# Layer 1's s1 of each edge's query as a 513th column of the gathered q row, instead of a broadcast through DRAM, and column sums over one column in 32

## Chip, cores and metric

One core of a Trainium2 chip runs the kernel. The metric is the time of one execution on the device in microseconds, as the median of several runs. TensorE (PE) multiplies matrices, VectorE (DVE), ScalarE (ACT) and GpSimd (POOL) work on tiles in SBUF, SyncE (SP) and POOL issue DMAs, and 16 DMA engines move the data.

## What is computed

Two graph layers on 32 batches of 512 nodes with 512 features, in float32. One adjacency matrix serves all batches; an entry is 1 with probability 1/128, so a node has about four neighbours. Layer 0 is attention with 8 heads of 64 over a node's neighbours; layer 1 is additive attention.

```python
    # layer 0
    h = jnp.maximum(_layernorm(x, axis=-1), 0.0)
    q, k, v = (h @ W + b for each), split into 8 heads
    attn = softmax(q k^T / 8 where adj, else -1e9);  x = x + (attn v) @ Wo + bo
    # layer 1
    h = jnp.maximum(_layernorm(x, axis=-1), 0.0) @ W
    s1, s2 = h @ a[:512], h @ a[512:]
    e = leaky_relu(s1[:, :, None] + s2[:, None, :], 0.2) * adj
    x = x + elu(softmax(e) @ h + beta * h)
```

Layer 1's softmax runs over all 512 nodes, and where adj is 0 the exponent is 0. So each row is the plain sum of all h (weight 1 each) plus, for the few edges, h weighted by exp(e) - 1.

## The kernel before

**Tiles.** A batch has T = 4 tiles of P = 128 nodes, sorted by the number of neighbours, so that the edges of a tile fill NG = 4 groups of 128 edge slots. For each group of slots the kernel gathers by indirect DMA (issued on POOL) one row for each edge: from a table `tab` in DRAM the neighbour's k, v and, for layer 1 of the batch two before (LAG = 2), the neighbour's s2 and normed features hn (`kv<-tab`, L925; a row is 1552 floats); and from `qtab` the query's q row (`qe<-qtab`, L945; 512 floats). Matrices of 0 and 1 (`OH`) with 32 columns a group bring sums over edges back to nodes.

**Layer 0, for a tile.** `qe` is multiplied by the k part (L976), summed over heads (L979), exponentiated (L985), and v is weighted by it on ACT (L990). PE sums edges to nodes (`px<-kv,OH`, L963), DVE divides (L1014), four transposes (L731) and the product with Wo (L41) follow, then the residual (L1029), the norm, relu into `hx` (L750), and two dot products with the rows of a (L1037): s2 into column 0 of `hx`, which goes to `tab` of the batch two later (L1043), and s1 into a column of the tile `s1`.

**self_sums, once a batch** (L1049). PE adds up `hx` over nodes with weights of 1/32 in 32 columns, so that each sum stands 32 times (L1057), ACT copies that (L1061), PE turns it (L731), and DVE adds up 128 columns for each quarter of the features (L1063, 128x512 to 128x4). For s1, PE turns the tile `s1` (L1066), ACT copies it (L1068), SP writes 512 floats to DRAM (`row`, L1069) and reads them back on all 128 partitions (`q<-row`, L1074) into a buffer of the ring `q`. DVE then picks each edge's s1: a product with OH (L1078) and a sum over 32 columns (L1079) give `s1e`, a column for each of the 16 groups of the batch.

**Layer 1's weights** (`edge_weights`, two batches later). DVE adds `s1e` and the gathered s2 for each half of the groups (L1095), applies the leaky slope (L1098), ACT takes exp (L1100), DVE subtracts 1 (L1101), copies it into the slots (L1105) and spreads it over OH (L1107, `wv`); PE sums with it (`pd<-kv,wv`, L963).

**Stage A, six tiles ahead.** x is fetched, normed, turned; k and v of two tiles come from seven half products (L837), and q from `queries`: product with Wq (L41), bias on DVE (L784), and a store by SP (L876). In batch 0 plain products make k and v (L802 to L811), and q, k and v are stored by indirect DMAs on POOL (L878), which need the nodes' places, worked out at the start.

**Order.** `Plan` builds the list of all operations once, each with an engine, an estimated duration, a due time (`key`; a tile is S = 20 units) and the buffers that it reads and writes. `Plan.order` then simulates the engines: at each step it takes, on the engine that can start first, the ready operation with the lowest key; an operation that needs a ring buffer waits for a free one, and rings other than PSUM's are handed out in order of key. PE gets a small bias to stay with the same width of weights (`STAY`), and DMAs are modelled as one pipe. The order that comes out is written down for each engine, and engines run it strictly in order. So a buffer less, a duration or a dependency more can move operations elsewhere. Rings that matter here: `q` 2 (also used for `q<-row`), `k` 2, `qe` 2 (both used by each tile), `kv` 5, `s1` 2.

Of the kernel before, what the change touches and what calls it, by code (L numbers as in the profile page):

```python
# [33 lines left out]
ROW = HO + HW_  # L34
LAG = 2
# [180 lines left out]
def kernel(  # L216
# [49 lines left out]
    def ring(n, shape, name):  # L266
# [8 lines left out]
        "q": ring(2, [P, D], "q"),  # L275
        "k": ring(2, [P, D], "k"),
        "v": ring(5, [P, H, VW], "v"),
        "kv": ring(5, [P, 2, ROW], "kv"),
        "qe": ring(2, [P, 2, D], "qe"),
# [12 lines left out]
        "s1": ring(2, [P, T], "s1"),  # L292
# [7 lines left out]
        "qtab": [dram.tile([N + 1, D], F32, name=f"qtab{i}", tag=f"qtab{i}") for i in range(3)],  # L300
# [27 lines left out]
    def setup():  # L328
        nc.gpsimd.iota(OH.bitcast(I32), pattern=[[1, D]], base=1, channel_multiplier=0)
        nc.gpsimd.iota(idx[:, 0, 0:1], pattern=[[1, 1]], base=0, channel_multiplier=1)  # L330
        make_identity(nc, ident)
        nc.gpsimd.memset(mhalf, -0.5)
        nc.vector.memset(rings["qe"][-1], 0.0)
        nc.vector.memset(one32, 1.0 / G)
        for b in rings["hx"]:
            nc.vector.memset(b[:, D:], 0.0)
        for b in rings["v"]:
            nc.vector.memset(b[:, :, HD:], 0.0)
        for b in [rmax, dmax, fin]:
            nc.vector.memset(b, 0.0)  # L340

    def constants():

        def load(fn, dma=4096, w=()):
            op("SP", 0.1, 20.0, fn, w=w, dma=dma)

        for dst, src in ((bk_r, bk), (bq_r, bq)):
            load(lambda dst=dst, src=src: nc.sync.dma_start(dst, bcast_rows(src, D)), P * D * 4, [C_["rows"]])
        load(lambda: nc.sync.dma_start(beta_b, bcast_rows(beta, 1)))
        zero = rings["qe"][-1].rearrange("p a b -> p (a b)")  # L350
        for tag, n in (("tk", D), ("tkv", D), ("qtab", D), ("th", HW_), ("tab", ROW)):
            for tab in rings[tag]:
                for c0, c1 in ((0, D), (HO, ROW)) if tag == "tab" else ((0, n),):
                    m = 1 if tag == "qtab" else DUMMY
                    load(lambda tab=tab, c0=c0, c1=c1, m=m: nc.sync.dma_start(
                        tab[N:, c0:c1], zero[:m, : c1 - c0]))
        for dst, src in ((bq_c, bq), (bk_c, bk)):
            load(lambda dst=dst, src=src: nc.sync.dma_start(
                dst, bass.AP(tensor=src.tensor, offset=src.offset, ap=[[1, P], [P, C]]),
                allow_slow_non_contiguous=True))  # L360
# [418 lines left out]
    def queries(b, t, key, hT):  # L779
# [4 lines left out]
        op("DVE", 0.7, key, lambda: nc.vector.tensor_tensor(q.ap, p.ap, bq_r, op=ALU.add), r=[p, C_["rows"]], w=[q])  # L784
# [128 lines left out]
    def stage_b(b):  # L913
# [16 lines left out]
        for t in range(T):  # L930
# [11 lines left out]
            if s is not None:  # L942
                qs = [buf("qe", f"qe{b}_{t}_{i}") for i in range(2)]
                for g in range(NG):
# [4 lines left out]
                       r=[s["qtab"], C_["qidx"]], w=[(qs[g // 2], g % 2)], dma=P * D * 4)  # L949
            wvb = edge_weights(b - LAG, t, kb, slots, held) if old is not None else None  # L950
# [17 lines left out]
    def layer0(b, t, kb, slots, held, qs, weights):  # L968

        s = st[b]  # L970
        for i in range(2):
# [3 lines left out]
            def mult(qe=qe, sl=sl):  # L975
                nc.vector.tensor_tensor(qe.ap, qe.ap, sl.ap[:, :, KO : KO + D], op=ALU.mult)  # L976

            def total(qe=qe, sb=sb):
                nc.vector.tensor_reduce(  # L979
                    sb.ap, qe.ap.rearrange("p n (h f) -> p n h f", f=HD), axis=AX.X, op=ALU.add  # L980
                )
# [10 lines left out]
            op("DVE", 1.24, key, mult, r=use([sl], [held[i]], "K"), w=[qe])  # L992
            op("DVE", 1.2, key, total, r=[qe], w=[sb])
# [55 lines left out]
    def self_sums(b, key):  # L1049
# [5 lines left out]
        def col_sums():  # L1055
# [5 lines left out]
        op("ACT", 0.6, key, lambda: nc.scalar.copy(csr.ap, pc.ap), r=[pc], w=[csr])  # L1061
        op("PE", 0.45, key + 0.49 * S, lambda: turned(pt.ap, csr.ap), r=[csr], w=[pt])
        op("DVE", 0.69, key + 0.5 * S, lambda: nc.vector.tensor_reduce(  # L1063
            cs.ap, pt.ap.rearrange("p (c q) -> p c q", c=C), axis=AX.X, op=ALU.add), r=[pt], w=[cs])
# [9 lines left out]
        op("SP", 0.1, key, lambda: nc.sync.dma_start(s1b.ap, row.ap.unsqueeze(0).to_broadcast([P, N])),  # L1074
           r=[row], w=[s1b], dma=P * N * 4)

        def pick():
            nc.vector.tensor_tensor(s1b.ap, OH, s1b.ap, op=ALU.mult)  # L1078
            nc.vector.tensor_reduce(  # L1079
                s1e.ap.rearrange("p t g -> p (t g)"), s1b.ap.rearrange("p (s r) -> p s r", r=G), axis=AX.X, op=ALU.add  # L1080
            )

        op("DVE", 1.4, key + 0.8 * S, pick, r=[C_["OH"]], w=[s1b, s1e])
        op("DVE", 0.2, key + 0.9 * S, lambda: nc.vector.scalar_tensor_tensor(
            fin, s["mv1"].ap[:, :, 0:2], 0.0, fin, op0=ALU.mult, op1=ALU.add), r=[s["mv1"]], w=[C_["fin"]])
        op("DVE", 0.2, key + 0.9 * S, lambda: nc.vector.tensor_tensor(rmax, rmax, s["rd"].ap, op=ALU.max),
           r=[s["rd"]], w=[C_["rmax"]])

    def edge_weights(b, t, kb, slots, held):
# [4 lines left out]
        for i in range(2):  # L1094
            op("DVE", 0.2, k1, lambda i=i: nc.vector.tensor_tensor(  # L1095
                z.ap[:, 2 * i : 2 * i + 2], s["s1e"].ap[:, t, 2 * i : 2 * i + 2], slots[i].ap[:, :, HO], op=ALU.add),
               r=[s["s1e"], *use([slots[i]], [held[i]], "H")], w=[z])
# [318 lines left out]
```

## Time and profile before

| | |
|---|---|
| runs shown | 2753.82, 2757.61, 2750.27 us; median 2753.82 |
| profiled execution | 2739.4 us, of which the span of the program 2737.2 |
| instructions in the span | 40002 |
| DMA | 242339 packets, 796.71 MB, mean 291 GB/s |
| granted TensorE clock | 0.988 in the mean |

How to read it: busy time is that of an engine's instructions without waits. Matmuls are pipelined and their ends modelled, so one product's duration (0.6 us for 128x512) is longer than the distance to the next one's start (0.43 us). "Idle before" is time of an engine ahead of an instruction, with what ended it. A line number is that of the kernel before. In a timeline line: start, duration, engine, line, operation, output and inputs, count.

### The profile page before, as it was taken

What the parts mean: (1) busy time and instruction counts of PE and PEld (TensorE: products, weight loads), DVE (VectorE), ACT (ScalarE), POOL (GpSimd) and SP (SyncE); (2) the same over time, 40 slices, a digit from 0 to 9 for tenths busy, and PEclk for the clock granted to TensorE, in tenths of its full rate; (3) what the DMA queues carried; (4) which work ended last, traced back from release to release, by engine and by line L of the source; (5) the groups of instructions that cost most, each with busy time, mean ns of one, the idle gap of its engine ahead of it and who ended that gap; (6) DMA issues with size and microseconds to landing.
All of it is one profiled execution on the core that took longest, in us unless ns stands there. A gap on an engine that the chain in (4) does not pass through costs nothing.

```text
span 2737.2 us, 40002 instructions
## 1 busy us (share of the span) xinstructions
PE 2662.8 (97%) x10250; PEld 1213.1 (44%) x10250; DVE 2093.0 (76%) x5138; ACT 1937.7 (71%) x6241; POOL 1835.0 (67%) x1730
## 2 busy tenths in 40 slices
PE   8899999999999999999999999999999999999986
PEld 4344444444444444444444444444444444444332
DVE  7667777777878777877877787777787787787763
ACT  1565777777778777777777777777777777777763
POOL 3787667666767676766766666666666676665663
PEclk9999999999999999999999999999999999999988
DMA  5889889888889888888888988988888898888963
GB/s 182 217 278 325 289 299 318 290 302 313 306 293 331 288 297 317 303 304 298 309 305 291 324 297 295 323 287 305 318 299 299 302 308 307 296 315 286 305 209 111
DMA packets 242339, 796.71 MB, mean 291 GB/s; under 512 B 35587, under 2 KB 35715, under 8 KB 242102
## 3 DMA queue, kind: packets, MB, share of 16 engines
q0 software_dynamic: 157056, 643.94, 69.8%
q1 hardware_dynamic: 85046, 150.15, 14.9%
q8 instruction: 83, 1.36, 0.2%
q14 instruction: 154, 1.26, 0.1%
HBM read 624.70 MB, written 169.26 MB: 290 GB/s over the span
## 4 chain that ended last, share of the span: by engine, by line
PE 91%; ACT 2%; DMA 2%; issue 2%; POOL 1%; DVE 1%; SPq 0%; POOLq 0%; DVEq 0%; ACTq 0%
PE pd L41 48%; PE pd L837 26%; PE pd L731 6%; PE pd L963 4%; PE px L963 4%; ACT kv L990 1%; DMA qe<-qtab,qidx 1%; PE pd L897 1%; PE pd L1057 1%; POOL kv L925 1%; DMA x<-in_x_dram,perm 0%; DMA kv<-tkv,idx 0%; POOL qe L945 0%; ACT hx L750 0%; DMA x<-in_adj_dram 0%
## 5 line engine op out<-in xcount | busy, mean ns | idle before, releaser
L990 ACT ACTIVATE kv<-kv 128x64 f32<-128x64 f32 x4096 | 1009.6, 335 | 6.0
L945 POOL DMA_INDIRECT qe<-qtab,qidx x512 | 544.7, 1064 | 245.2 <-issue 104.9
L925 POOL DMA_INDIRECT kv<-tab,idx x480 | 518.9, 1081 | 175.8 <-issue 111.0
L41 PE MATMUL pd<-wo,oT 128*128 128x512 f32 x1032 | 476.2, 605 | 6.0 <-ACT oT L1027 5.8
L41 PE MATMUL pd<-w,gT 128*128 128x512 f32 x1024 | 465.4, 597 | 4.0 <-ACT gT L1148 4.0
L41 PE MATMUL pd<-wq,hT 128*128 128x512 f32 x1024 | 465.1, 597 | 0.0
L756 POOL DMA_INDIRECT x<-in_x_dram,perm x252 | 355.6, 1411 | 82.6 <-issue 48.4
L976 DVE TENSOR_TENSOR qe<-qe,kv 128x1024 f32<-128x1024 f32 x256 | 312.0, 1221 | 30.8 <-DMA qe<-qtab,qidx 13.9
L41 PEld LDWEIGHTS pd<-wo,oT 128*128 128x128 f32 x1032 | 198.5, 194 | 254.1 <-issue 228.5
L979 DVE TENSOR_REDUCE s<-qe 128x16 f32<-128x1024 f32 x256 | 310.3, 1214 | 0.9
L41 PEld LDWEIGHTS pd<-w,gT 128*128 128x128 f32 x1024 | 195.4, 192 | 249.8 <-issue 235.1
L41 PEld LDWEIGHTS pd<-wq,hT 128*128 128x128 f32 x1024 | 195.6, 192 | 246.4 <-issue 244.5
L761 POOL DMA_INDIRECT out_dram<-w,perm x128 | 139.1, 1087 | 185.7 <-DVE w L1163 133.8
L743 POOL TENSOR_TENSOR mv<-mv,mhalf 128x1 f32<-128x1 f32 x256 | 176.0, 689 | 126.0 <-DVE mv L740 89.8
L837 PE MATMUL pd<-wk,hT 128*128 128x512 f32 x496 | 238.6, 606 | 1.4 <-ACT hT L776 1.4
L837 PE MATMUL pd<-wt,S 128*128 128x512 f32 x496 | 237.6, 601 | 1.6 <-DVE k L845 0.9
L837 PE MATMUL pd<-wv,S 128*128 128x512 f32 x496 | 233.3, 593 | 0.2 <-DVE v L845 0.2
L1157 ACT ACTIVATE w<-pd,dn 128x512 f32<-128x512 f32 x128 | 87.5, 684 | 152.4 <-PE pd L41 152.1
L1029 DVE TENSOR_TENSOR x<-pd,x 128x512 f32<-128x512 f32 x128 | 88.2, 689 | 129.6 <-PE pd L41 123.5
L738 DVE BATCH_NORM_STATS2 st<-x 128x6 f32<-128x512 f32 x256 | 176.5, 689 | 7.4 <-DMA x<-in_x_dram,perm 3.4
L1037 DVE CUSTOM_DVE_ANT_0 w<-hx,wa_r 128x512 f32<-128x512 f32 x256 | 175.9, 687 | 4.9 <-ACT hx L750 3.9
L731 PE MATMUL pd<-ident,w 128*128 128x128 f32 x1152 | 154.2, 276 | 25.6 <-DVE w L1014 14.0
(201 smaller groups left out, 3579.4 us busy)
## 6 DMA issues: line engine op xcount, KB each, us to landing
qtab<-q SPq DMA_DIRECT2D x124, 256.0 KB
tab<-hx SPq DMA_DIRECT2D x120, 260.0 KB
tab<-v SPq DMA_DIRECT2D x120, 260.0 KB
tab<-k SPq DMA_DIRECT2D x120, 256.0 KB
qe<-qtab,qidx POOLq DMA_INDIRECT x512, 6.7
q<-row SPq DMA_DIRECT2D x32, 256.0 KB
kv<-tab,idx POOLq DMA_INDIRECT x480, 7.7
x<-in_x_dram,perm POOLq DMA_INDIRECT x252, 7.3
```

The source lines that it names most:

```text
L41: nc.tensor.matmul(out, lhsT, rhs, start=start, stop=stop)
L731: nc.tensor.transpose(p[:, ts(c, P)], src[:, ts(c, P)], ident)
L738: nc.vector.bn_stats(s6.ap, src.ap)
L743: op("POOL", 0.75, key, lambda: nc.gpsimd.tensor_tensor(mv.ap[:, t, 2:3], mv.ap[:, t, 2:3], mhalf[:, 0:1], op=ALU.pow), w=[(mv, t)])
L756: nc.gpsimd.indirect_dma_start(dst, None, rows, bass.IndirectOffsetOnAxis(ap=perm[:, t : t + 1], axis=0), **lim)
L837: nc.tensor.matmul(p.ap, lhs()[:, c, :], rhs[:, c, :], start=first and c == 0, stop=c == K2 - 1, skip_group_check=True)
L925: nc.gpsimd.indirect_dma_start(dst, None, tab.ap, bass.IndirectOffsetOnAxis(ap=idx[:, t, g : g + 1], axis=0), bounds_check=N + DUMMY - 1, ...
L945: op("POOL", 1.3, kb - 0.84 * S + 0.1 * g, lambda q=qs[g // 2], g=g, t=t: nc.gpsimd.indirect_dma_start(q.ap[:, g % 2, :], None, s["qtab"]. ...
L963: nc.tensor.matmul(out(g), lhs(g), slots[g // 2].ap[:, g % 2, c0 : c0 + n], start=True, stop=True)
L976: nc.vector.tensor_tensor(qe.ap, qe.ap, sl.ap[:, :, KO : KO + D], op=ALU.mult)
L979: nc.vector.tensor_reduce(sb.ap, qe.ap.rearrange("p n (h f) -> p n h f", f=HD), axis=AX.X, op=ALU.add)
L990: nc.scalar.activation(p[:, h, 0:HD], p[:, h, 0:HD], AF.Copy, scale=p[:, h, HD : HD + 1])
```

## The change

`queries` of batch b copies a column of `s1` of batch b - 2 beside q, so that a row of `qtab` has 516 floats (q, s1, three unused zeros), and the gather that brings an edge's q brings its s1 too. `edge_weights` adds that column instead of `s1e`. The last two batches, whose layer 1 runs with no layer 0 beside it, keep the old way (`spread_s1`, a function of its own). The plan's bookkeeping treats q and the s1 column of a gathered row as parts. Ring `k` has one buffer instead of two, `s1` three instead of two. `self_sums` scales the column sums by 32 in ACT's copy and then takes one column in 32, 16 in all, for the sum. The two small operations on `fin` and `rmax` stand earlier in the text, with the same keys.

```diff
+QW = 516
-        "q": ring(2, [P, D], "q"),
-        "k": ring(2, [P, D], "k"),
+        "q": ring(2, [P, QW], "q"),
+        "k": ring(1, [P, D], "k"),
-        "qe": ring(2, [P, 2, D], "qe"),
+        "qe": ring(2, [P, 2, QW], "qe"),
-        "s1": ring(2, [P, T], "s1"),
+        "s1": ring(3, [P, T], "s1"),
-        "qtab": [dram.tile([N + 1, D], F32, ...
+        "qtab": [dram.tile([N + 1, QW], F32, ...
...
-        op("DVE", 0.7, key, lambda: nc.vector.tensor_tensor(q.ap, p.ap, bq_r, op=ALU.add), r=[p, C_["rows"]], w=[q])
+        op("DVE", 0.7, key, lambda: nc.vector.tensor_tensor(q.ap[:, 0:D], p.ap, bq_r, op=ALU.add), r=[p, C_["rows"]], w=[(q, "q")])
+        if b >= LAG:
+            s1 = st[b - LAG]["s1"]
+            op("DVE", 0.1, key, lambda: nc.vector.tensor_copy(q.ap[:, D : D + 1], s1.ap[:, t : t + 1]),
+               r=[(s1, t)], w=[(q, "s1")])
...
-            op("DVE", 1.24, key, mult, r=use([sl], [held[i]], "K"), w=[qe])
-            op("DVE", 1.2, key, total, r=[qe], w=[sb])
+            op("DVE", 1.24, key, mult, r=[(qe, "use"), *use([sl], [held[i]], "K")], w=[qe.q])
+            op("DVE", 1.2, key, total, r=[(qe, "use"), qe.q], w=[sb])
...
-        op("ACT", 0.6, key, lambda: nc.scalar.copy(csr.ap, pc.ap), r=[pc], w=[csr])
+        op("ACT", 0.6, key, lambda: nc.scalar.activation(csr.ap, pc.ap, AF.Copy, scale=float(G)), r=[pc], w=[csr])
-        op("DVE", 0.69, key + 0.5 * S, lambda: nc.vector.tensor_reduce(
-            cs.ap, pt.ap.rearrange("p (c q) -> p c q", c=C), axis=AX.X, op=ALU.add), r=[pt], w=[cs])
+        op("DVE", 0.2, key + 0.5 * S, lambda: nc.vector.tensor_reduce(
+            cs.ap, pt.ap[:, 0 :: G].rearrange("p (c q) -> p c q", c=C), axis=AX.X, op=ALU.add), r=[pt], w=[cs])
+        if b + LAG >= B:
+            spread_s1(b, key)
...
+    def spread_s1(b, key):
...
         for i in range(2):
-            op("DVE", 0.2, k1, lambda i=i: nc.vector.tensor_tensor(
-                z.ap[:, 2 * i : 2 * i + 2], s["s1e"].ap[:, t, 2 * i : 2 * i + 2], slots[i].ap[:, :, HO], op=ALU.add),
-               r=[s["s1e"], *use([slots[i]], [held[i]], "H")], w=[z])
+            def add(i=i):
+                s1 = s["s1e"].ap[:, t, 2 * i : 2 * i + 2] if qs is None else qs[i].ap[:, :, D]
+                nc.vector.tensor_tensor(z.ap[:, 2 * i : 2 * i + 2], s1, slots[i].ap[:, :, HO], op=ALU.add)
+
+            op("DVE", 0.2, k1, add, r=[*([s["s1e"]] if qs is None else [(qs[i], "use"), qs[i].s1]),
+                                       *use([slots[i]], [held[i]], "H")], w=[z])
```

## The prediction

> **What bounds the kernel now.** I read the page first, then the busy times by stretch, then TensorE's timeline in one late batch, then the waits of the tiles that the change touches.
>
> ```profile
> PE 2662.8 (97%) x10250; PEld 1213.1 (44%) x10250; DVE 2093.0 (76%) x5138; ACT 1937.7 (71%) x6241; POOL 1835.0 (67%) x1730
> PE 91%; ACT 2%; DMA 2%; issue 2%; POOL 1%; DVE 1%; SPq 0%; POOLq 0%; DVEq 0%; ACTq 0%
> ```
>
> TensorE is busy 97% of the span and carries 91% of the chain that ended last. A share of the whole span can hide stages, so the stretches come next (time; then busy us of PE, PEld, DVE, ACT, POOL; then clock, DMA share, GB/s).
>
> ```profile
> 0.00:100.00 100.00, 85.00 (x255) 41.82 (x256) 73.43 (x216) 24.02 (x49) 46.85 (x53) 0.93 0.60 171
> 200.00:300.00 100.00, 93.59 (x352) 40.72 (x351) 71.51 (x168) 60.60 (x199) 70.26 (x68) 0.98 0.89 309
> 1500.00:1800.00 300.00, 300.00 (x1208) 138.35 (x1200) 237.62 (x577) 222.54 (x713) 204.22 (x193) 1.00 0.87 302
> 2500.00:2600.00 100.00, 93.04 (x373) 40.81 (x372) 71.23 (x174) 71.67 (x241) 62.70 (x58) 0.95 0.87 297
> 2600.00:2680.00 80.00, 64.63 (x254) 27.23 (x253) 52.16 (x148) 51.08 (x163) 51.62 (x48) 0.89 0.69 208
> 2680.00:2737.00 57.00, 35.13 (x116) 13.88 (x114) 18.13 (x61) 17.34 (x41) 18.95 (x19) 0.85 0.31 94
> ```
>
> From 1500 to 1800 TensorE has no idle time. All its idle time is 2737.2 - 2662.8 = 74 us: 26.7 before 300 (15.0 + 5.3 + 6.4), 44.2 after 2500 (7.0 + 15.4 + 21.9), about 3 between. So work taken off any other engine can be felt in two places, the start and the tail; between them only TensorE's own work and its order count.
>
> Order counts because products with 32 columns of weights (L963, L897, L1057) and full ones do not follow each other for free. The first L1057 of each batch marks a period: from 1097.6 to 2473.9, 17 batches, each is 80.96 us within 0.02, with 8 changes between the two kinds. The batches from 362.2 to 608.3 last 81.7 to 82.3 us with 12 changes. A change costs about (82.0 - 80.96) / 4 = 0.26 us.
>
> **What is removed, added and moved.** The sum is made against the profiled execution (2739.4 us, span 2737.2); the median of the runs shown, 2753.8, is 14.4 above it, and I put the difference on the median.
>
> *TensorE.* For 30 of 32 batches the transpose of s1 goes.
>
> ```profile
> L1066 PE MATMUL pd<-ident,s x32: 271/272/273, 196.0 to 2668.4; 128*4 128x128 f32 x32
> 1098.62 0.27 PE L1066 MATMUL pd<-ident,s 128*4 128x128 f32 x1
> 1098.72 0.60 PE L731 MATMUL pd<-ident,x 128*128 128x128 f32 x4
> ```
>
> Its duration of 0.27 us is not what it costs: the next product starts 0.10 to 0.11 us later, products being pipelined. 30 x 0.11 = **-3.3 us**, on the path, since TensorE is full around each.
>
> *VectorE.* Gone: 30 picks of 0.685 + 0.686 (L1078, L1079), 41.1 us; and 32 sums of hn, 0.684 each, now over 16 columns instead of 512. The nearest row for that is L613's reduction of 256 columns, 0.42, and a 128x4 operation, 0.16: I take 0.2, so 32 x 0.48 = 15.5 us. Added: 120 copies of one column, 0.16 by L1105's copy of two columns: 19.2. Net -37 us of 2093, worth nothing between 300 and 2500, where PE does not wait for DVE.
>
> *ScalarE, SyncE.* 30 copies of 0.25 and 60 DMA issues go, 30 of which make SP's queue wait for the row to land (90.0 us in all). The scaled copy of the column sums (L1061) stays at L904's 0.60 against 0.59. Nothing, under the same cover; if the cover went, ACT at 71% has room.
>
> *DMA.* 30 broadcasts of 256 KB go, 7.9 MB of 796.7. All 640 stores and gathers of q carry 16 B more a row: 1.3 MB. What a gathered row of 2064 B costs is not in the trace. In one early stage rows of 2048 B (kv<-tk) land after 5.7 us and rows of 2080 B (kv<-tv) after 5.6, so nothing is one end; the other is a tenth more on the q gathers, the gap between the 6.7 us of a qe gather and the 7.4 of the kv gathers with their threefold rows. I take nothing, by the nearer row. TensorE's cover here is thick: a qe gather is followed by its product on DVE 4 to 15 us after it has landed.
> Against the change speaks the Trainium skill, DMA: Bandwidth & Descriptors, How a descriptor splits into AXI transactions: a read that does not start on a 256 B boundary fetches from the boundary below it. By that a row at a step of 2064 B takes an estimated 68.5 beats of 32 B on average instead of 64, 7% more on the q gathers; the sum stays as it is as long as the cover holds.
>
> *The new wait.* The z additions (L1095) now read the q buffer, so they wait for the qe gather too, and the next gather into that buffer waits for them. Behind them in DVE's order stand exp, L1101, L1105 and L1107, and then PE's L963. In the late batches this is free: the four tiles of the batch at 1101 make their second addition at 1126.5, 1150.4, 1164.7 and 1191.4, and their last gather, issued 6.7 us before it lands, is there at 1121.9, 1134.8, 1163.0 and 1175.7. The weights are ready 10 to 19 us before PE takes them. In batches 2 to 9 the additions run up to 9.3 us ahead of the gather, and the slack behind them is 2 to 20 us; in seven tiles it is short, by 0.1 to 4.8, together 12. PE has other products there, so this changes order, not work. Nor does the added column wait: L784 writes q 16 to 19 us after the L1037 that makes its s1 (1095.1 against 1076.7). One buffer for k holds too: a k is stored at 1115.45 and the next written at 1124.74, 9.3 us for a store whose like, the gathers, land in 7.7.
>
> In those nine batches, 362.2 to 1097.6, the time over nine periods of 80.96 is 735.4 - 728.6 = 6.8 us. The new order may save all of it or add as much. DVE's 2 us less a batch brings px earlier, and a z that comes later moves its product towards px, which saves changes. I take **-1**, with -6.8 and +6.8 for ends.
>
> *Start.* With one k buffer the second key product cannot start before the first k is stored.
>
> ```profile
> 25.16 3.60 PE L41 MATMUL pd<-wk,hT 128*128 128x512 f32 x8
> 33.24 0.67 DVE L806 TENSOR_TENSOR k<-pd,bk_r 128x512 f32<-128x512 f32 x1
> 35.25 1.12 POOL L878 DMA_INDIRECT tk<-k,posi  x1 [0.30 <-DVE mv L740]
> 84.29 1.12 PE L731 MATMUL pd<-ident,x 128*128 128x128 f32 x4 [5.47 <-ACT x L750]
> ```
>
> Issued at 35.25, it lands about 36.4 + 2.7 (qtab<-q) = 39.1. PE can put forward what follows, two value products, one query product (3.43 each) and 0.9: 25.2 + 11.2 = 36.4, a hole of 2.7 us. The third and fourth key products follow at links of 3.43 + 0.67 + 1.0 + 2.8, with queueing 9.5: 48.6 and 58, instead of 40.2 and 50.6. The last k then lands near 67; gathers begin at 69.0 and in earnest at 73.2, so they hardly move. PE's displaced work can fall into the 5.5 us for which it waits at 84.29. From 0 to +8 (a hole of 2.7 at each of three links); I take **+1.5**.
>
> *Tail.* The pick of batch 29 (1.37 us at 2573) and half a sum stand among DVE work for which PE waits 1.3, 1.9 and 1.5 us. From -1.9 to 0: **-0.8**.
>
> Sum: -3.3 - 1 + 1.5 - 0.8 = -3.6, 2753.8 - 3.6 = **2750.2 us**. Its own ends: -3.3 - 6.8 + 0 - 1.9 = -12 and -3.3 + 6.8 + 8 + 0 = +11.5. Under 0.3% (8.3 us) a measurement of this kernel can't tell from no change.
>
> **Rivals.**
> *It settles late, or never* (slower). The batches from 10 on keep the 12 changes of the early ones, because z or the single k buffer keeps L963's two products apart: +0.7 to +1.35 a batch over 20 batches is +14 to +27; with -3.3 and +1.5, 2766 to 2779. It decides once weights come over 10 us later than now. For it: the seven short tiles, and an order made afresh. Against: in the late batches z does not move at all.
> *It settles at once* (faster): -3.3 - 6.8 - 1.9 = -12, 2742. For it: DVE and DMA get lighter in the early batches. Against: the wait for qe falls in just these.
> *The gathers of q bound* (slower): DMA is at 0.87 of its engines; q gathers move 134 of 797 MB, so a tenth more on them is 1.7% of 0.87, far from full. Only rows that cost twice would do it, 0.87 x 1.17 = 1.02: 2% of 2754, 2809.
> *Nothing but new order*: the gain of 3.3 is lost at the start; 2754, inside my forecast.
>
> **Numbers.** Forecast (within 8.3 us, 2745.5 to 2762): 0.57. Settles at once, 0.20. Settles late, 0.20; gathers bound, 0.03. So faster 0.20, same 0.57, slower 0.23. The range reaches from 2740, beyond the quick rival, to 2772, the middle of the late one, which leaves out under 2 in 10.
>
> **What would show it.** Right: L1066 twice, PE without idle from 300 to 2500, batch periods of 80.85, the second wk product near 39. Wrong: late periods of 81.5 or more, L963's two products apart in late batches, PE waiting for z, or idle before 100 well over 15 us. DVE near 2056 busy checks the rest of the count.

## The result

The changed kernel takes 2755.99 us (median of 14 runs, 2748.01 to 2763.45), the kernel before 2754.47 in runs of the same series (14 runs, 2750.27 to 2757.87): ratio **1.0004, 95% interval 0.9994 to 1.0014**. No difference can be measured. The forecast, 2750.2 us and "within 0.3%", lies 5.8 us under it.

The profiled execution of the changed kernel took 2756.4 us, its span 2754.4, 17 us more than the span of before (2737.2). Nearly all of that does not come back: a second profile of each, taken one after the other on one chip (`before_2`, `after_2` below), gives spans of 2745.5 and 2746.5. A single execution of one kernel moves by more than the change does, and so does a series on another chip: in the four series of runs here, the kernel before has medians of 2754.5, 2745.6, 2745.8 and 2738.2. So kernels are compared below by the ratio to before's runs in the same series, and traces by their pattern.

Line numbers have moved: L41 is now L42 (products), L731 L734 (transposes), L837 L844 (half products), L963 L973 (sums over edges), L1057 L1067 (column sums). On the changed kernel's page, the busy times and the chain of work that ended last:

```profile
PE 2669.4 (97%) x10220; PEld 1219.0 (44%) x10220; DVE 2039.1 (74%) x5200; ACT 1923.9 (70%) x6211; POOL 1816.7 (66%) x1730
PE 90%; DVE 3%; issue 2%; DMA 1%; ACT 1%; POOL 1%; another core or an unknown queue 0%; SPq 0%; POOLq 0%; DVEq 0%; ACTq 0%
```

30 PE instructions and 54 us of VectorE are gone; PE is as full as before, and busy for 6.6 us longer. That is not more work but a lower granted clock, 0.985 in the mean against 0.988: at the start and in the tail there are stretches at half clock, 82 us of them here and 65 in the profile of before, and in them a product of 128x512 starts 0.853 us after the one before it instead of 0.429. The busy times by stretch of the same execution (time; PE, PEld, DVE, ACT, POOL; clock, DMA share, GB/s):

```profile
0.00:100.00 100.00, 86.18 (x251) 42.21 (x252) 73.59 (x218) 23.94 (x48) 44.13 (x52) 0.93 0.62 168
200.00:300.00 100.00, 94.43 (x350) 41.37 (x349) 67.89 (x158) 62.17 (x211) 67.53 (x66) 0.97 0.86 296
1500.00:1800.00 300.00, 299.54 (x1182) 137.75 (x1181) 229.08 (x582) 220.98 (x711) 199.12 (x191) 1.00 0.87 296
2500.00:2600.00 100.00, 92.35 (x375) 40.99 (x373) 72.51 (x175) 78.15 (x264) 65.47 (x59) 0.98 0.88 299
2600.00:2680.00 80.00, 64.51 (x247) 29.49 (x247) 56.19 (x160) 54.36 (x175) 51.02 (x48) 0.83 0.75 235
2680.00:2754.00 74.00, 50.72 (x174) 20.48 (x174) 25.34 (x84) 25.25 (x62) 29.16 (x29) 0.87 0.37 111
```

Against before: in the first 100 us PE is busy for 1.2 us longer, not less; from 1500 to 1800 PE now has half a us of gaps where it had none.

The table cuts each trace at the first product of the column sums of batches 2, 11 and 29 (counted from 0). "Gaps" is the time between 300 and 2500 us in which no product runs, which is a sum over all gaps, small ones too; "changes" is between products with 32 columns of weights and full ones, per batch. I counted both from the records of the trace.

| us | start (to batch 2) | batches 2-10 | batches 11-28 | from batch 29 | gaps | late periods, changes |
|---|---|---|---|---|---|---|
| before | 362.2 | 735.4 | 1457.2 | 182.3 | 3.3 | 80.96, 8 |
| before_2 | 364.4 | 738.6 | 1461.4 | 181.2 | 8.0 | 80.96, 8; some up to 82.3 |
| after | 372.9 | 730.5 | 1465.4 | 185.6 | 6.3 | as after_2, more scatter |
| after_2 | 367.5 | 730.3 | 1464.5 | 184.2 | 5.0 | 80.90, 80.91, 81.72, 81.78 in turn; 8, 8, 10, 8 |

So the time is the same, but not its parts: against before_2, +3.1 in the start, **-8.3** in batches 2-10, **+3.1** in batches 11-28 (+7.3 against the profile without scatter), +3.0 in the tail. The early batches settle to 8 changes at once, where before needed until batch 7. The late batches lose it again, in a cycle of four that both profiles of the changed kernel show (in `after`, single batches last up to 0.3 longer).

In a short batch of the cycle, the two sums over edges of one tile (L973 twice, weights of 128x32) stand together, here on TensorE's timeline in after_2:

```profile
1400.51 1.07 PE L973 MATMUL pd<-kv,wv 128*32 128x512 f32 x8
1401.39 1.06 PE L973 MATMUL px<-kv,OH 128*32 128x260 f32 x16
1402.38 1.98 PE L844 MATMUL pd<-wt,S 128*128 128x512 f32 x4
1404.20 1.88 PE L844 MATMUL pd<-wv,S 128*128 128x512 f32 x4
```

In the third batch of the cycle, four full products come between them, two changes of width more:

```profile
1474.07 1.02 PE L844 MATMUL pd<-wk,hT 128*128 128x512 f32 x2
1475.02 1.07 PE L973 MATMUL pd<-kv,wv 128*32 128x512 f32 x8
1476.02 1.98 PE L844 MATMUL pd<-wk,hT 128*128 128x512 f32 x4
1477.93 1.09 PE L973 MATMUL px<-kv,OH 128*32 128x260 f32 x16
1478.95 0.70 PE L844 MATMUL pd<-wt,S 128*128 128x512 f32 x1
```

From start to start, the four full products between the sums take 1.91 us, where four products with a full one on either side take 4 x 0.43 = 1.72, and the first sum takes 1.00 instead of 0.88. So the two extra changes cost about 0.3 us. That batch is 0.8 us longer than 80.91 and the next one 0.9; most of it is waiting, in that batch at the transposes and in the next one at the half products:

```profile
1463.55 1.09 PE L734 MATMUL pd<-ident,x 128*128 128x128 f32 x8
1464.91 1.31 PE L734 MATMUL pd<-ident,w 128*128 128x128 f32 x8 [0.27 <-DVE w L1024]
1515.05 3.60 PE L844 MATMUL pd<-wk,hT 128*128 128x512 f32 x8
1518.82 1.98 PE L844 MATMUL pd<-wt,S 128*128 128x512 f32 x4 [0.17 <-issue]
```

Eight transposes at 0.109 us take 0.87; the first eight here take 1.36 from start to start and, with the next product at 1466.24, the second eight 1.33. Eight half products at 0.43 take 3.43 and here 3.77. Added up by the starts of all products of the two batches, about 1.3 of the 1.7 us that a cycle loses are waits. The brackets show less (0.27 and 0.17), because the modelled end of a product reaches into the wait behind it; so "gaps" in the tables is a lower bound.

### The profile page after: what moved, and what is told of

It reads as the page before. It is cut to its first block, busy times and chain, and to the rows that moved or that the text cites. A ratio compares the mean times of both kernels' runs of the same rounds, so it can differ in the third digit from the quotient of the medians.

```text
span 2754.4 us, 39777 instructions
## 1 busy us (share of the span) xinstructions
PE 2669.4 (97%) x10220; PEld 1219.0 (44%) x10220; DVE 2039.1 (74%) x5200; ACT 1923.9 (70%) x6211; POOL 1816.7 (66%) x1730
## 3 DMA queue, kind: packets, MB, share of 16 engines
q8 instruction: 83, 1.36, 0.2%
## 4 chain that ended last, share of the span: by engine, by line
PE 90%; DVE 3%; issue 2%; DMA 1%; ACT 1%; POOL 1%; another core or an unknown queue 0%; SPq 0%; POOLq 0%; DVEq 0%; ACTq 0%
PE pd L42 47%; PE pd L844 27%; PE pd L734 7%; PE pd L973 4%; PE px L973 4%; PE pd L904 1%; PE pd L1067 1%; DMA qe<-qtab,qidx 1%; ACT kv L1000 1%; POOL kv L932 1%; DVE qe L986 0%; DVE w L1156 0%; DVE s L989 0%; DVE st L741 0%
## 5 line engine op out<-in xcount | busy, mean ns | idle before, releaser
L954 POOL DMA_INDIRECT qe<-qtab,qidx x512 | 521.5, 1019 | 251.0 <-issue 125.3
L932 POOL DMA_INDIRECT kv<-tab,idx x480 | 531.8, 1108 | 193.2 <-issue 132.8
L42 PE MATMUL pd<-wo,oT 128*128 128x512 f32 x1032 | 476.4, 605 | 2.6 <-ACT oT L1037 2.4
L42 PE MATMUL pd<-w,gT 128*128 128x512 f32 x1024 | 467.0, 599 | 3.5 <-ACT gT L1167 2.4
L42 PE MATMUL pd<-wq,hT 128*128 128x512 f32 x1024 | 464.8, 597 | 0.3 <-issue 0.3
L759 POOL DMA_INDIRECT x<-in_x_dram,perm x252 | 362.9, 1440 | 88.9 <-issue 60.7
L42 PEld LDWEIGHTS pd<-wo,oT 128*128 128x128 f32 x1032 | 198.1, 194 | 247.2 <-issue 225.5
L42 PEld LDWEIGHTS pd<-w,gT 128*128 128x128 f32 x1024 | 196.1, 192 | 250.2 <-issue 231.3
L42 PEld LDWEIGHTS pd<-wq,hT 128*128 128x128 f32 x1024 | 195.5, 192 | 245.1 <-issue 241.4
L764 POOL DMA_INDIRECT out_dram<-w,perm x128 | 146.3, 1143 | 235.1 <-DVE w L1182 208.2
L844 PE MATMUL pd<-wt,S 128*128 128x512 f32 x496 | 240.0, 606 | 2.5 <-ACT x L753 1.8
L844 PE MATMUL pd<-wk,hT 128*128 128x512 f32 x496 | 237.8, 605 | 3.4 <-issue 2.1
L844 PE MATMUL pd<-wv,S 128*128 128x512 f32 x496 | 233.3, 593 | 0.0
L746 POOL TENSOR_TENSOR mv<-mv,mhalf 128x1 f32<-128x1 f32 x256 | 153.7, 608 | 83.9 <-DVE mv L743 53.3
L734 PE MATMUL pd<-ident,w 128*128 128x128 f32 x1152 | 159.5, 280 | 37.9 <-DVE w L1024 19.5
L734 PEld LDWEIGHTS pd<-ident,w 128*128 128x128 f32 x1152 | 133.7, 143 | 116.7 <-issue 53.2
```

Of the source, the lines that this page charges most:

```text
L42: nc.tensor.matmul(out, lhsT, rhs, start=start, stop=stop)
L734: nc.tensor.transpose(p[:, ts(c, P)], src[:, ts(c, P)], ident)
L759: nc.gpsimd.indirect_dma_start(dst, None, rows, bass.IndirectOffsetOnAxis(ap=perm[:, t : t + 1], axis=0), **lim)
L844: nc.tensor.matmul(p.ap, lhs()[:, c, :], rhs[:, c, :], start=first and c == 0, stop=c == K2 - 1, skip_group_check=True)
L932: nc.gpsimd.indirect_dma_start(dst, None, tab.ap, bass.IndirectOffsetOnAxis(ap=idx[:, t, g : g + 1], axis=0), bounds_check=N + DUMMY - 1, ...
L954: op("POOL", 1.3, kb - 0.84 * S + 0.1 * g, lambda q=qs[g // 2], g=g, t=t: nc.gpsimd.indirect_dma_start(q.ap[:, g % 2, :], None, s["qtab"]. ...
```

## The experiments

**Theories.** *Order*: TensorE is full, the work that the change removes is nearly all hidden, and what the time does follows from the order that `Plan` writes, which shifts with any change of work or buffers. *New wait*: the z additions now wait for the gather of q. *Buffer*: the single k buffer costs the start. *Lighter engines*: VectorE and DMA work is worth something, and another cost hides it.

**Second looks at both kernels.** No edit.

> The kernel before once more, for a second profile. The profiled execution of before (2739.4 us) lies below all 14 timed runs (2750.3 to 2757.9), while the changed kernel's (2756.4) lies at its median. If that first profile was a lucky one, this one has a span of 2748 to 2756 us and the extra time sits in the first 300 us, with late batches again at 80.96 us. If the changed kernel is really 17 us slower, this one has a span near 2737 again.

> The changed kernel once more, for a second profile. Order theory: the late batches repeat the cycle of four (80.9, 80.9, 81.7, 81.8 us) to within 0.1, since the order is written down; the stalls before 150 us (5.5 us at 110 and 5.6 at 138), if they are of one execution alone, are gone or elsewhere.

Measured: 2747.84 and 2748.46 us in their profiled executions; before's median in this series is 2745.61. The span of before_2, 2745.5, lies between the two that I had expected, and only 2.2 of its 8.3 us more are in the start. The rows are in the table above. The late batches of before_2 are those of before with single hiccups of 0.9 to 1.1 us (82.07, 82.04, 81.81); the cycle of after_2 is that of after. So the cycle belongs to the order, and the 17 us between the first two profiles are not a steady difference.

**no_s1: less work alone.** In before, the way of s1 (transpose, copy, two transfers, picks) is left out for batches 0 to 29.

```diff
-        ps, s1t, row = buf("D", "ps1"), buf("wv", f"s1t{b}"), buf("row", f"row{b}")
+        if b + LAG >= B:
+            ps, s1t, row = buf("D", "ps1"), buf("wv", f"s1t{b}"), buf("row", f"row{b}")
...
-                z.ap[:, 2 * i : 2 * i + 2], s["s1e"].ap[:, t, 2 * i : 2 * i + 2], slots[i].ap[:, :, HO], op=ALU.add),
+                z.ap[:, 2 * i : 2 * i + 2], (s["s1e"].ap if s["s1e"] else nzE)[:, t, 2 * i : 2 * i + 2], slots[i].ap[:, :, HO], op=ALU.add),
```

> Before, with the whole way of s1 left out for batches 0 to 29 (no transpose, copy, row through DRAM or pick; layer 1's weights read a constant tile in place of s1, so s1 is left out of them) and nothing put in its place. It bounds from below what the change could bring, with two k buffers and no wait for q. Order theory (TensorE full; the transpose is worth 0.05 us a batch, the rest is what order the planner finds): within 6 us of before, -6 to +6. Theory that the new wait or the single k buffer eats a real gain of the removed work: 8 us or more faster than before.

Measured: ratio **1.0053 (1.0037 to 1.0069)**, slower with less work and nothing put in its place. That is some 14 us, outside the -6 to +6 that I had given the order theory too. Start 356.5, batches 2-10 743.0, batches 11-28 1465.8, gaps 15.9.

**no_wait: the changed kernel without the new wait.** z adds a constant tile instead of the gathered column.

```diff
-                s1 = s["s1e"].ap[:, t, 2 * i : 2 * i + 2] if qs is None else qs[i].ap[:, :, D]
+                s1 = s["s1e"].ap[:, t, 2 * i : 2 * i + 2] if qs is None else nzE[:, t, 2 * i : 2 * i + 2]
```

> The changed kernel with one edit: the z additions read a constant tile in place of the gathered s1 column (s1 is left out of layer 1's weights), so they wait for the kv gather alone and do not hold the q buffer; the column is still written, stored and gathered. Theory of the new wait: late batches return to 80.9 us each and the time falls by 7 us against the changed kernel. Order theory: the late batches change to some other cycle, 80.9 to 81.5 in the mean, and the time stays within 5 us of the changed kernel.

Measured: ratio **1.0053 (1.0034 to 1.0072)**, gaps 11.9, batches 11-28 1467.1. Here, too, the loss is larger than I had allowed (within 5 us of the changed kernel). Taking the wait away did not help; it made another order, which was worse. So this run alone does not clear the wait. The traces of the changed kernel do: in after and after_2 VectorE sits idle before none of the 240 additions that read the gathered column, and TensorE waits for layer 1's weights once (0.7 us at 333) in after and never in after_2. The new wait falls as a direct cause of the late loss.

**k1: the single k buffer alone**, in before.

```diff
-        "k": ring(2, [P, D], "k"),
+        "k": ring(1, [P, D], "k"),
```

> The kernel before with one edit: k has one buffer instead of two, as in the changed kernel. Nothing of layer 1 uses k, so from the third batch on the order should be that of before. If the single buffer costs what the changed kernel lost at its start, the first product of the column sums of batch 2 moves from 362-364 us (the two profiles of before) to 366-370 us (after: 372.9, after_2: 367.5), batches 2-10 and 11-28 keep 736-739 and 1457-1462 us, and the time is 0.1 to 0.25% over before. If the start's loss has another source (wider gathers, the moved dots, the work on the q row), the mark stays within 2 us of before's and the time within 0.1%.

Measured: ratio **0.9997 (0.9984 to 1.0009)**; the mark of batch 2 at 364.4, batches 11-28 1459.5. It costs nothing that can be measured. Of its 7.9 us of gaps, 4.9 are two waits, of 3.3 and 1.6 us. The order did not fall back to before's from the third batch on, as I had expected: it differs in many places up to batch 10 and from batch 11 on in one, eight products with Wo four products earlier.

**cols: the sums over four columns alone**, in before, with the planner told 0.2 us instead of 0.69.

```diff
-        op("ACT", 0.6, key, lambda: nc.scalar.copy(csr.ap, pc.ap), r=[pc], w=[csr])
+        op("ACT", 0.6, key, lambda: nc.scalar.activation(csr.ap, pc.ap, AF.Copy, scale=float(G)), r=[pc], w=[csr])
-        op("DVE", 0.69, key + 0.5 * S, lambda: nc.vector.tensor_reduce(
-            cs.ap, pt.ap.rearrange("p (c q) -> p c q", c=C), axis=AX.X, op=ALU.add), r=[pt], w=[cs])
+        op("DVE", 0.2, key + 0.5 * S, lambda: nc.vector.tensor_reduce(
+            cs.ap, pt.ap[:, 0 :: G].rearrange("p (c q) -> p c q", c=C), axis=AX.X, op=ALU.add), r=[pt], w=[cs])
```

> The kernel before with the sums of hn taken over the four columns of a tile instead of all 128, and s1 still brought by the broadcast through DRAM. It takes some 0.5 us of VectorE out of each batch, 15 us of busy time in all, and nothing from TensorE. If VectorE's work mattered, the time would fall by up to 0.5%. By the theory that TensorE is full and only the order of its products is left, the time does not follow the work removed: the late batches get another cycle with another number of changes of weight width, and the time ends anywhere from 0.3% under to 0.5% over before; a late period other than 80.96 us with more than 8 changes, or with holes, shows it.

Measured: ratio **1.0065 (1.0049 to 1.0082)**, a little beyond the upper end that I gave. Its late batches have 8 changes, as in before, and last 81.0 to 83.4 us. So a reading of the loss as one of changes of width would be too narrow: here it is holes. TensorE's waits from 300 to 2500 us in cols (operation, what it waited for: us in total, times, longest), the largest four:

```profile
PE pd L41 <- ACT oT L1027: 7.0, 8, 1.0
PE pd L731 <- ACT w L1061: 4.6, 5, 1.4
PE pd L731 <- DVE w L1014: 3.2, 4, 1.2
PE pd L837 <- ACT v L859: 1.5, 1, 1.5
```

**before_order and after_order: the same instructions in another order.** Planner constants, and in after_order also the due time of layer 1's weights; the constants reckon with faster transfers and, for some engines, other lags.

```diff
 before_order
-    STAY, WAIT = 1.0, 0.3
-    FREE = 5.0
+    STAY, WAIT = 3.0, 0.1
+    FREE = 8.0
-    LAG = {"PE": 0.25, "DVE": 0.12, "ACT": 0.2, "POOL": 0.15, "SP": 0.0}
+    LAG = {"PE": 0.25, "DVE": 0.08, "ACT": 0.25, "POOL": 0.15, "SP": 0.0}
-                dma_free = max(dma_free, t + o.us + 2.2) + o.dma / 300e3
+                dma_free = max(dma_free, t + o.us + 2.2) + o.dma / 320e3
 after_order
-    STAY, WAIT = 1.0, 0.3
+    STAY, WAIT = 4.0, 0.2
-    LAG = {"PE": 0.25, "DVE": 0.12, "ACT": 0.2, "POOL": 0.15, "SP": 0.0}
+    LAG = {"PE": 0.25, "DVE": 0.1, "ACT": 0.15, "POOL": 0.15, "SP": 0.0}
-                dma_free = max(dma_free, t + o.us + 2.2) + o.dma / 300e3
+                dma_free = max(dma_free, t + o.us + 2.2) + o.dma / 320e3
-        k1 = kb + 0.6 * S
+        k1 = kb + 0.45 * S
```

> The kernel before with five constants of its planner changed (how long TensorE stays on a kind of product, what it waits for one, when a buffer counts as free, two lags, the transfer rate it reckons with): every instruction, buffer and transfer is kept, only the order in which they are written differs. If the order decides, the time moves as much as the change under study moves its parts: 0.3 to 0.8% under before, with the gain in batches 11-28 (under 1455 us) or at the ends. If what the instructions cost decides, it stays within 0.2%.

> The changed kernel with five constants of its planner changed, its work, buffers and transfers kept. The order was chosen so that every late batch has 8 changes of weight width on TensorE instead of the cycle 8, 8, 10, 8 of the changed kernel. By the order theory the late period falls from 81.33 to about 80.9 us, batches 11-28 from 1465 to about 1457 us, and the whole to 0.3 to 0.8% under before. If the late loss comes from the change itself (the wider gathers, the wait of the z addition for the gathered column, the single k buffer), the late period stays at 81.3 us and the time within 0.2% of before.

Measured: ratios **1.0050 (1.0034 to 1.0067)** and **1.0139 (1.0116 to 1.0162)**. Both expectations missed in sign, though not in kind: an order alone moves the time by 0.5% and 1.4%. after_order has 8 changes in every batch, as planned, and takes 28 us more than after in batches 11-28 (1493.5; gaps 31.5). Its waits from 300 to 2500 us, the largest three:

```profile
PE pd L844 <- ACT v L866: 10.3, 14, 2.0
PE pd L844 <- ACT v L868: 9.9, 16, 1.3
PE pd L734 <- DVE w L1024: 4.6, 7, 1.0
```

With a planned lag of 0.15 us for ScalarE the planner put half products (L844), which add onto a PSUM tile that ScalarE first copies out (L866, L868), so close behind these copies that on the chip the copy is late. (That it was this lag, of the constants changed, was not tried alone.) What matters, then, is both: few changes, and room between a result and its reader.

**cols_fixed: the edit of cols in the order of before.** As cols, but the planner still reckons 0.69.

```diff
 cols, with
-        op("DVE", 0.2, key + 0.5 * S, lambda: nc.vector.tensor_reduce(
+        op("DVE", 0.69, key + 0.5 * S, lambda: nc.vector.tensor_reduce(
```

> The kernel before with the sums of hn over four columns, as in cols, but the planner still reckons 0.69 us for them, so that every instruction stands where it stood before. If it was the order that made cols 0.65% slower, this one falls back to before's time: within 0.15% of it, late period 80.96 us with 8 changes, VectorE's busy time 15 to 18 us under 2093. If the edit itself costs time (the scaled copy on ScalarE, the strided read), it stays 0.5 to 0.65% over before, like cols.

Measured: ratio **0.9997 (0.9988 to 1.0006)**, span 2736.5, late periods 80.96, gaps 3.1. The same edit cost 0.65% where the planner knew of it and nothing where it didn't. The two ran on different chips, each against runs of before on its own; the mean granted clock is 0.988 for both and for both sets of before, so it isn't the clock. On TensorE, VectorE, ScalarE and GpSimd the instructions of cols_fixed stand in the order of before. The busy times on the page of cols_fixed, VectorE 15.4 us under before:

```profile
PE 2661.3 (97%) x10250; PEld 1214.1 (44%) x10250; DVE 2077.6 (76%) x5138; ACT 1937.6 (71%) x6241; POOL 1825.6 (67%) x1730
```

Its group of the reduction (out and in shapes, count; busy us, mean ns; idle before and what ended it):

```profile
L1063 DVE TENSOR_REDUCE cs<-pd 128x4 f32<-128x16 f32 x32 | 5.3, 167 | 2.9 <-PE pd L731 2.8
```

Each sum takes 0.167 us instead of 0.684, 16.5 us of VectorE in all, and the time does not notice.

**all_fixed: the work of the whole change in the order of before.** Single k buffer, q rows of 516 floats, sums over four columns, no way of s1; the planner keeps before's costs, and the operations of the s1 way stay in its list but issue nothing.

```diff
+QW = 516
-        "q": ring(2, [P, D], "q"),
-        "k": ring(2, [P, D], "k"),
+        "q": ring(2, [P, QW], "q"),
+        "k": ring(1, [P, D], "k"),
...
+        late = b + LAG >= B
...
-        o = op("PE", 0.15, key + 0.485 * S, lambda: nc.tensor.transpose(ps.ap[0:T, 0:P], s["s1"].ap, ident), r=[s["s1"]], w=[ps])
+        o = op("PE", 0.15, key + 0.485 * S, lambda: late and nc.tensor.transpose(ps.ap[0:T, 0:P], s["s1"].ap, ident), r=[s["s1"]], w=[ps])
```

> The work of the whole change in the order of before: the way of s1 (transpose, copy, two transfers, picks) leaves no instruction for batches 0 to 29, the q rows are 516 floats wide, k has one buffer, the sums are over four columns; the planner reckons with before's costs. It leaves out the dots' values: z takes a constant tile in place of s1, and the added column of q is never written. If the work counts as I summed it, TensorE gains 30 transposes at 0.05 to 0.11 us (1.6 to 3.3) and a little of the ends, and nothing else is felt: 0.05 to 0.25% under before, late period 80.90 us. If lighter DVE and DMA were worth more and only the new order hid it, it is over 0.3% under before; if the wider rows cost, it is over before and the late period above 81.

Measured: ratio **0.9984 (0.9975 to 0.9993)**, 4.4 us of 2754; late periods 80.90 and 80.91; gaps 0.1. My sum was -3.6. Its order on TensorE is that of k1, product for product, not quite that of before; k1 in this order has 0.9997. Two things of the change are not in it: the 120 copies of s1 (17 us of VectorE) and z's wait. Nor is the granted clock held: it is 0.9895 in the mean over the runs of all_fixed and 0.9882 for before, and 0.0013 of 2738 us is an estimated 3.6 us, less what of it falls where TensorE is idle. So 4.4 us is the work's own worth only together with a clock that differed; in the late batches, where the clock is full, the work is worth 0.05 us a batch.

**after_new and before_new: both kernels, one other set of constants, with longer lags.**

```diff
-    STAY, WAIT = 1.0, 0.3
+    STAY, WAIT = 1.5, 0.15
-    LAG = {"PE": 0.25, "DVE": 0.12, "ACT": 0.2, "POOL": 0.15, "SP": 0.0}
+    LAG = {"PE": 0.35, "DVE": 0.2, "ACT": 0.3, "POOL": 0.15, "SP": 0.0}
```

> The changed kernel with only the planner's lags (PE 0.35, VectorE 0.2, ScalarE 0.3 instead of 0.25, 0.12, 0.2) and its STAY and WAIT (1.5, 0.15 instead of 1.0, 0.3) altered: longer lags leave more room between a result and its reader, where the last reordering took that room away and put TensorE in wait for ScalarE's evictions. By the order theory there is a gain in it that the changed kernel's order does not take: 8 changes in every late batch and no waits, batches 11-28 at 1450 to 1458 us, the whole 0.3 to 1% under before. If any departure from before's order costs, as three of the runs so far would also allow, it is 0.3% or more over before.

> The kernel before with the same five constants as after_new. By the order theory it gains too, 0.1 to 0.6% under before, and the distance between it and after_new is what the change is worth when both have an order that suits them: I expect after_new 0.1 to 0.4% ahead (the transposes' 1.6 to 3.3 us, a few us of the start and tail). If any departure from before's order costs, it is 0.3% or more over before.

Measured: **0.9961 (0.9947 to 0.9974)** for the changed kernel, 2726.56 us where before takes 2738.24; **1.0009 (1.0000 to 1.0018)** for before. The first is faster than before, where the changed kernel is not: the change with another order. The second is a miss: the kernel before has nothing to gain from these constants.

| us | start | batches 2-10 | batches 11-28 | from batch 29 | gaps | ratio |
|---|---|---|---|---|---|---|
| cols_fixed | 361.3 | 735.1 | 1457.2 | 182.9 | 3.1 | 0.9997 |
| all_fixed | 365.0 | 732.2 | 1456.3 | 180.4 | 0.1 | 0.9984 |
| before_new | 369.0 | 732.8 | 1457.8 | 178.6 | 2.5 | 1.0009 |
| after_new | 370.7 | 725.6 | 1456.7 | 171.8 | 2.8 | 0.9961 |
| k1 | 364.4 | 741.3 | 1459.5 | 180.4 | 7.9 | 0.9997 |
| no_wait | 363.6 | 737.2 | 1467.1 | 185.3 | 11.9 | 1.0053 |
| no_s1 | 356.5 | 743.0 | 1465.8 | 183.7 | 15.9 | 1.0053 |
| before_order | 360.7 | 740.7 | 1478.9 | 181.2 | 17.2 | 1.0050 |
| cols | 368.5 | 742.1 | 1472.7 | 180.0 | 18.9 | 1.0065 |
| after_order | 364.7 | 741.3 | 1493.5 | 181.5 | 31.5 | 1.0139 |

The first four ran on one chip. The ratio follows the gaps roughly: up to 8 us of them, it lies between 0.9961 and 1.0009; from 12 to 19, 0.5 to 0.65% over; at 31, 1.4% over. Neither k1's buffer, nor less work (no_s1, cols), nor no wait (no_wait) lines up with it. Among the first four, the gaps do not order the ratios.

The tail of after_new is 8.6 us shorter than that of all_fixed. The last stretches of after_new, columns as above:

```profile
2600.00:2680.00 80.00, 63.78 (x264) 28.15 (x263) 51.95 (x157) 50.79 (x158) 54.47 (x50) 0.94 0.69 214
2680.00:2750.00 70.00, 26.82 (x100) 10.89 (x100) 15.88 (x54) 15.27 (x38) 16.09 (x16) 0.92 0.21 65
```

The same of all_fixed:

```profile
2600.00:2680.00 80.00, 67.04 (x264) 27.76 (x263) 49.90 (x149) 48.96 (x154) 51.81 (x48) 0.91 0.68 206
2680.00:2750.00 70.00, 31.53 (x102) 12.77 (x101) 16.69 (x54) 16.15 (x39) 16.31 (x16) 0.86 0.22 66
```

After 2680 us, 26.8 us of products are left where all_fixed has 31.5, but that is not work taken forward: behind the mark of batch 29 both traces have the same 528 products and the same idle time of TensorE (44.3 and 44.2 us). What differs is the granted clock, 0.94 and 0.92 in these rows against 0.91 and 0.86: the stretches at half clock add up to 26 us in the tail of after_new and to 41 in that of all_fixed. Whether the order brings these stretches about is not shown: over the runs, the mean clock is 0.990 for after_new and 0.9895 for all_fixed, and one run of after_new took 2725.8 us at 0.989. From batch 29 on TensorE has room in any order (over 30 us of its idle time lies after 2500 us in every kernel above).

## Why the prediction was right, step by step

The class was right and the time 5.8 us off, in part by luck. Between the second profiles, the early batches gave more than I had summed, and the start, the late batches and the tail took it back. The late batches had no term for order, and the granted clock had no term at all.

- **The sum, -3.6: near in all_fixed, by luck.** all_fixed measures -4.4 (-1.9 to -6.9). But the largest part, the transposes, is worth half of what I took, and the start and the tail moved with the clock (below).
- **Transposes, -3.3: mis-sized, about -1.6.** 30 are gone, as counted. But in one order with and without them (k1 and all_fixed), the late period falls from 80.96 to 80.905, 0.05 us each and not 0.11. TensorE's timeline around one of them, in a late batch of cols_fixed:

```profile
1905.96 1.04 PE L1057 MATMUL pd<-hx,one 128*32 128x512 f32 x8
1906.93 0.27 PE L1066 MATMUL pd<-ident,s 128*4 128x128 f32 x1
1907.04 0.60 PE L731 MATMUL pd<-ident,x 128*128 128x128 f32 x4
1907.48 1.47 PE L731 MATMUL pd<-ident,w 128*128 128x128 f32 x12
```

The same place in all_fixed, where the transpose of s1 is not there:

```profile
1906.25 1.04 PE L1060 MATMUL pd<-hx,one 128*32 128x512 f32 x8
1907.22 0.66 PE L734 MATMUL pd<-ident,x 128*128 128x128 f32 x4
1907.71 1.47 PE L734 MATMUL pd<-ident,w 128*128 128x128 f32 x12
```

  From the column sums to the twelve transposes it is 1.52 us with L1066 and 1.46 without. L1066 takes 0.11, but the four transposes behind it take 0.44 with it and 0.49 without: the first transpose behind the 32-column products is stretched by 0.06 (0.167 instead of 0.109 to the next start), and with L1066 in between it isn't.
- **A change of width, 0.26: too high.** I had it from whole batches, 82.0 against 80.96 us. By the starts of the products in after_2 a pair of changes costs 0.3 us, so about 0.16 each; the rest of the difference between early and late batches is waits and products that stand on the other side of a mark.
- **Order in batches 2-10, -1 with ends of -6.8 and +6.8: the sign and place right, the size at its end.** -5.1 against the first profile of before, -8.3 against the second. Some 2 us of it is not time won: four full products and four transposes that before has in these batches stand ahead of the mark of batch 2. It settled at once, as the quick rival had it.
- **Batches 11-28, no term for order: this step failed.** I took the late batches as settled because z does not move there, and expected periods of 80.85. They come to 81.36 in the mean: +7.3 over 18 batches against the undisturbed profile. Each cycle of four lasts 325.3 us where four of all_fixed's batches last 323.6. It is waits for the most part and one pair of changes of width, as shown above. Nothing in the work makes it so: all_fixed has 80.905 in the same batches, and after_new, with every part of the change in it, 80.90 in all but the first few.
- **Start, +1.5 with ends of 0 and +8: inside the ends, by another mechanism.** after_2 is +3.1 against before_2, all_fixed +3.7 against cols_fixed, but k1, the buffer alone, has its mark where before_2 has it (364.4; before's medians in the two series are 2745.8 and 2745.6) and 0.9997 in all. The hole of 2.7 us does not come up: PE's timeline in after has the second key product at 36.70 (39 predicted) and no gap before it.

```profile
29.83 3.60 PE L42 MATMUL pd<-wq,hT 128*128 128x512 f32 x8
33.27 3.60 PE L42 MATMUL pd<-wv,hT 128*128 128x512 f32 x8
36.70 3.60 PE L42 MATMUL pd<-wk,hT 128*128 128x512 f32 x8
```

  The third and fourth stand at 49.85 and 65.72 (48.6 and 58 predicted), and idle time before 100 us is 13.8 us against 15.0. Other products were put forward. Up to the mark of batch 2 TensorE is idle for 31.1 us in after_2 and 32.5 in before_2, so no hole made the mark later: 2.2 us more of products stand ahead of it, and the stretches at half clock add up to 27 us against 17. all_fixed and cols_fixed have the same idle time there (29.3 and 29.4 us) and 24 against 20 us at half clock.
- **Tail, -0.8: wrong in after; the sign in all_fixed is luck.** after_2 has +3.0 against before_2, with the same busy time and 47.6 us idle instead of 44.6. all_fixed has -2.5 against cols_fixed, but with the same idle time (44.2 and 44.4 us), so not by the waits that I meant; its stretches at half clock add up to 41 us instead of 48.
- **VectorE at nothing: shown.** cols_fixed takes 16 us off it for 0.9997. The count: picks -41.1, sums -16.7, copies +17.4 (0.145 each), together -40 against my -37. The page's total falls by 54. Of the other 14, 10 are overlap: the durations of all VectorE instructions add up to 44 us less, and the page counts time in which two of them run only once. In the changed kernel:

```profile
L790 DVE COPY q<-s 128x1 f32<-128x1 f32 x120 | 17.4, 145 | 0.0
L1073 DVE TENSOR_REDUCE cs<-pd 128x4 f32<-128x16 f32 x32 | 5.2, 163 | 1.3 <-PE pd L734 1.3
```

- **DMA at nothing: right by the packets, and by the late periods of all_fixed (80.905), which has the wider rows.** A packet of two rows of 2064 B, nearly all of them q rows, takes 160 ns in the median in the trace of after_2, one of two rows of 2048 B takes 159 in before_2. The Trainium skill, DMA: Bandwidth & Descriptors, How a descriptor splits into AXI transactions, gave by its rule of 256 B boundaries an estimated 7% on these gathers; the measurement decides, and it is 0.6%.
- **The new wait at nothing: right.** VectorE never sits idle for it in after and after_2, and after_new has it and is the fastest kernel here. What removing it is worth in a held order was not run.
- **Rivals.** *Settles late* did not come: no batch of after has more than 10 changes. *Gathers bound* did not come. *Settles at once* came in the early batches, and its gain was given back. *Nothing but new order*, 2754, is what happened, with one correction: I let the gain be lost at the start, and as much again was lost in the late batches and in the tail each.
- **Signs.** The transpose of s1 runs twice, in the last two batches, as said. "Late periods of 81.5 or more, L963's two products apart" was named as a sign against, and half of it holds: 81.36 in the mean, and apart in one batch of four. "Without idle from 300 to 2500" did not come (gaps of 6.3 and 5.0 us), and only half of the late periods are near 80.85 (80.90). Idle time before 100 us did not rise. VectorE is busy for 2039 us, not 2056, for the reasons above.

What stays open: which decision of the planner starts the cycle of four was not traced, and no_s1 and no_wait were not run in a held order. The granted clock was not separated from the order: its mean is 0.9864 over the 14 runs of the changed kernel, 0.9882 to 0.9887 for before in the other three series, and 0.990 for after_new, and 0.002 of 2750 us is an estimated 5.5 us, as much as the differences here. Nor is all of after_new's 0.23% over all_fixed the change's: it is an order found for it, and before_new shows only that the same constants don't do this for before.

## What to carry to other kernels

When one engine is full and a planner writes the order, an edit has two effects, its work and the reshuffle; price the first from rows, and give the second its own range over every stage (here from 0.4% faster to 1.4% slower), the settled ones too. To tell them apart, run the edit once with the planner's old costs (the order held) and once with the new ones: here 0.9997 against 1.0065 for one and the same edit. After a change that removes work, tune the planner's constants again before judging it: for the changed kernel, a set with longer lags gave 0.9961 and one with shorter lags lost 1.4%; for before, the longer lags gave nothing (1.0009). And compare the granted clock of the ends before a difference there is called work or order.

## What the runs showed of the hardware

- A change of weight width is paid on both sides of it. From start to start in after_2, the last full product (128x512) ahead of 32-column ones takes 0.523 us instead of 0.429, the last 32-column product (128x512) ahead of full ones 0.523 instead of 0.411, and the first full product behind it 0.533. A 128x128 transpose as the first one behind takes 0.165 to 0.167 instead of 0.109, so a small product placed there is nearly half free (0.05 of L1066's 0.11 us is left to save).
- At half clock, a 128x512 product starts 0.853 us after the one before instead of 0.429. Between 300 and 2500 us four of the traces have one such stretch of 3.4 us each (before_2, k1, no_s1, before_order), within 5 us after TensorE began to wait for 2.0, 3.3, 3.5 and 2.1 us; four other waits of 2.0 us were not followed by one, and no shorter wait there was.
- Rows of 2064 B are gathered at the pace of rows of 2048 B: 160 against 159 ns for two.
- TensorE that is 97% busy can lose 1.4% by waits of up to 2 us, none of which is large enough to be seen in busy shares: PE's share is 97% in all kernels here but after_order, where it is 96%.
- The same kernel in four series of runs has medians 0.6% apart (2738.2 to 2754.5), twice the difference that was to be told.
